# Attention's projections read a transposed copy of x; the layer norm moves into the weights and into row factors

## Chip, core and metric

The kernel runs on one core of one Trainium2 chip. The metric is the time of one execution on the device in microseconds (us), median of the runs shown. Five engines work side by side, each through its own list of instructions in order: PE (matrix products; PEld is its weight load), DVE (vector), ACT (scalar functions), POOL (the second vector engine) and SP (issues all DMAs here). They wait for each other by semaphores.

## The reference

x is 2 x 2048 x 512. The kernel computes one pre-norm block of a transformer:

```
x = x + attention(layernorm(x))      16 heads of 32, rotary positions, causal softmax, Wo
x = x + ffn(layernorm(x))            base_w and base_b, plus 8 low-rank experts, the best 2 of each row
layernorm(x) = (x - mean) / sqrt(var + 1e-5), by row
```

Queries, keys and values are layernorm(x) times Wq, Wk and Wv transposed; queries and keys are then turned by cosine and sine of the position.

## The kernel before

The 4096 rows are worked in 8 blocks of 512 rows (n = 0 to 7, `BLK`), four per batch; a block has four row tiles of 128 (t). The heads are worked in four groups of four (g); a group's 128 columns lie on 128 partitions. A step is one (block, group). In each step PE computes the scores of the next step once for the row maxima (`sm`, L410; reduced on DVE, L428) and the scores of the present step again, transposed (`sc`, L557), with the maxima subtracted by a small product (L581). ACT takes the exponential into `pt` (L597), PE multiplies with the values (`av`, L631), and POOL adds the `pt` tiles up for the row sums (L680). Three `pt` buffers rotate (`PTS`). The sums go through DRAM to be inverted and spread (L701 to L714).

Before a block's attention its projections are made ready by `prepare(n)`: `load` brings the four row tiles (L140) and the cosine and sine of the block (L148); `measured` takes mean and variance on DVE (L181 to L183), and the power -0.5 and the shift on POOL (L184, L185); `scaled` normalises on ACT (L189); `turned` transposes each tile on PE by four products with the identity into one PSUM bank (L195), and ACT copies it to `xnt_a` (L196). `project` (L225) makes one group's keys or queries from `xnt_a`: four products over the 128-row parts c of the weight; then DVE swaps pairs (L238) and multiplies with the cosine (L239), POOL multiplies the swapped with the sine (L240) and adds (L241). `value` (L250) makes one row tile's values, and ACT copies them per group (L258). `finish` does a block's output product, norm, experts and result.

The order on PE, ACT and DVE is the order in which the program emits it (`manual_schedule`, L65); POOL and SP are ordered by the tile framework's scheduler. A planner in the main loop (L864 to L920) counts phases, half a tile of keys for four heads each, some 3 us. `set_aside(at, do)` emits do at a phase; `wait(stage, at, not_before)` puts PE work in a list with a due phase, a cost in us and an earliest phase, which is emitted between attention's products when credit or due time says so. `start_block(n)` is called one block ahead and fixes these phases from the block's first phase `at`, `LEAD` (12, fewer behind a short block) and `EARLY` (14). In it, before the change:

```
set_aside(at - lead - EARLY + t, lambda t=t: load(t))
set_aside(at - lead - EARLY + 2 + t, lambda t=t: measured(t))
set_aside(at - lead - EARLY + 4 + t, lambda t=t: scaled(t))
wait([(0.5, lambda t=t: turned(t))], at - lead - 8 + t, at - lead - 9 + t)
```

Projections may be emitted from phase `at - lead - 6`. Behind blocks 0 and 4, whose causal part is one block wide, lead is 0. `xnt_a`, cosine and sine have one buffer each, the weights of `finish` one buffer `w` in turn, and the tag `tmp` six (row tiles, swapped pairs, sums).

Of the kernel before, what the change touches and what calls it, by code (L numbers as in the profile page):

```python
# [21 lines left out]
BLK = 512  # L22
NT = BLK // P
NB = S // BLK
NC = D // P
EPS = 1e-5
# [8 lines left out]
def preln_attention_moe_lora(  # L35
    ctx: ExitStack,
    tc: tile.TileContext,
    x: bass.AP,
    wq_t: bass.AP,
    wk_t: bass.AP,  # L40
    wv_t: bass.AP,
# [9 lines left out]
    nc = tc.nc  # L51
# [70 lines left out]
    one = const.tile([P, 1], F32, name="one")  # L122
# [3 lines left out]
    power = const.tile([P, 1], F32, name="power")  # L126
# [5 lines left out]
    blocks = [(b, j) for b in range(B) for j in range(NB)]  # L132
# [36 lines left out]
    def load_in_turn(src, name):  # L169
# [2 lines left out]
        nc.sync.dma_start(out=w, in_=src.rearrange("(c p) o -> p c o", p=P))  # L172
        return w

    def moments(xt, t, name):

        n6, n2 = nc.vector.BN_STATS_DIM, nc.vector.BN_AGGR_DIM
        made = small.tile([P, n6 + n2 + 2], F32, tag="mom", bufs=4, name=f"mom_{name}_{t}")
        st, mv = made[:, :n6], made[:, n6 : n6 + n2]
        rstd, shift = made[:, n6 + n2 : n6 + n2 + 1], made[:, n6 + n2 + 1 :]  # L180
        nc.vector.bn_stats(st, xt)  # L181
        nc.vector.bn_aggr(mv, st)
        nc.vector.tensor_scalar_add(rstd, mv[:, 1:2], EPS)  # L183
        nc.gpsimd.tensor_tensor(rstd, rstd, power, ALU.pow)  # L184
        nc.gpsimd.tensor_scalar(shift, mv[:, 0:1], rstd, -1.0, ALU.mult, ALU.mult)  # L185
        return rstd, shift

    def normalise(xn, xt, by):
        nc.scalar.activation(xn, xt, AF.Identity, bias=by[1], scale=by[0])  # L189
# [8 lines left out]
    def prepare(n):  # L198

        j = blocks[n][1]
        made = {"q": [], "k": [], "v": []}
        held = {"x": [], "by": []}

        def load(t):
            held["x"].append(first_x[t] if n == 0 else load_x(n, t, False))
            if t == NT - 1:
                held["turn"] = first_turn if n == 0 else load_turn(j)

        def measured(t):
            held["by"].append(moments(held["x"][t], t, f"a{n}"))

        def scaled(t):
            normalise(held["x"][t], held["x"][t], held["by"][t])

        def turned(t):
            if t == 0:
                held["xn_t"] = wide.tile([P, NC, BLK], F32, tag="xnt_a", name=f"xnt_a{n}")
            turn(held["x"][t], held["xn_t"], t, f"a{n}")  # L220

        def project(which, w, g):
            pj = bank(f"{which}ps_{n}_{g}")
            for c in range(NC):
                nc.tensor.matmul(  # L225
                    out=pj,
                    lhsT=w[:, c, bass.ts(g, P)],
                    rhs=held["xn_t"][:, c, :],
                    start=(c == 0),
                    stop=(c == NC - 1),  # L230
                )
            if which == "k":
                dest = kv.tile([P, BLK], F32, tag="k", name=f"k_{n}_{g}")
            else:
                dest = wide.tile([P, BLK], F32, tag="q", bufs=3, name=f"q_{n}_{g}")
            made[which].append(dest)
            sw = p2.tile([P, BLK], F32, tag="tmp", bufs=6, name=f"sw_{which}_{n}_{g}")
            nc.vector.stream_shuffle(sw, pj, SWAP)  # L238
            nc.vector.tensor_mul(dest, pj, held["turn"][0])  # L239
            nc.gpsimd.tensor_mul(sw, sw, held["turn"][1])  # L240
            nc.gpsimd.tensor_add(dest, dest, sw)  # L241

        def value(t):
            if t == 0:
                made["v"] += [
                    kv.tile([P, NT, P], F32, tag="v", name=f"v_{n}_{g}") for g in range(NC)
                ]
            pv = bank(f"vps_{n}_{t}")
            for c in range(NC):
                nc.tensor.matmul(  # L250
                    out=pv,
                    lhsT=held["xn_t"][:, c, bass.ts(t, P)],
                    rhs=wv[:, c, :],
                    start=(c == 0),
                    stop=(c == NC - 1),
                )
            for g in range(NC):
                nc.scalar.copy(made["v"][g][:, t, :], pv[:, bass.ts(g, P)])  # L258
# [6 lines left out]
        return (load, measured, scaled, turned), heads, [[(3.6, lambda t=t: value(t))] for t in range(NT)], made  # L265

    def finish(n, ctx_t):

# [542 lines left out]
    def set_aside(at, do):  # L811
        aside.append((at, do))
        aside.sort(key=lambda entry: entry[0])

    def wait(stage, at, not_before=0):
        waiting.append((at, len(waiting), not_before, stage))
        waiting.sort(key=lambda entry: entry[:2])

    def start_block(n):

        (load, measured, scaled, turned), heads, vals, made = prepare(n)
        keys[n], values[n], queries[n], contexts[n] = made["k"], made["v"], made["q"], []
        at = begin[NC * n]

        lead = min(LEAD, at - begin[NC * n - 1] - 6) if n > 0 else 0
        for t in range(NT):
            if n > 0:
                set_aside(at - lead - EARLY + t, lambda t=t: load(t))
                set_aside(at - lead - EARLY + 2 + t, lambda t=t: measured(t))
                set_aside(at - lead - EARLY + 4 + t, lambda t=t: scaled(t))  # L830
                wait([(0.5, lambda t=t: turned(t))], at - lead - 8 + t, at - lead - 9 + t)
            else:
                load(t)
        if n == 0:
            for do in (measured, scaled, turned):
                for t in range(NT):
                    do(t)
            make_masks_of_maxima()
        for g in range(NC):
            for i, stage in enumerate(heads[g]):  # L840
                if n == 0 and 2 * g + i < 3:
                    do_stage(stage)
                else:
                    here = begin[NC * n + g]

                    free = begin[NC * n + g - 1] + 3 if i else 0
                    wait(stage, here - 4 + i, max(free, at - lead - 6))
            if g == 1:
                for stage in vals:
                    wait(stage, begin[NC * n + 1] + 1, at - lead - 6)  # L850

    def end_block(n):

# [3 lines left out]
        for i, stage in enumerate(stages):  # L857
            wait(stage, start + (i + 1) * (end - start) / len(stages), start)

    EARLY, BEHIND, LEAD = 14, 3, 12  # L860
    start_block(0)
    before = turned = ending = None
    late = []
    for step in steps + [None]:  # L864
        maxima = []
        if step:
            n, g = step
# [15 lines left out]
        for i in range(slots):  # L883
# [3 lines left out]
            for _ in side_by_side(*todo):  # L887
                phase[0] += 1
                given = between()
# [12 lines left out]
                while available(phase[0]) is not None:  # L902
# [78 lines left out]
```

## Time and profile before

| | us |
|---|---|
| runs | 1808.67 median (1806.64 to 1812.35, 3 runs) |
| profiled execution, its own time | 1807.61 |
| its span, first to last instruction | 1805.6 |
| mean granted clock of TensorE | 0.993 |
| DMA bytes | 61.53 MB, 42284 packets |
| x transposed on PE (L195, 128 products) | 22.1 busy |
| x normalised on ACT (L189) / copied (L196) | 26.3 / 18.4 busy |
| power and shift on POOL (L184, L185) | 17.5 / 8.5 busy |
| POOL's additions of pt (L680) | 1093.0 busy |

Busy time is the time in which an engine had an instruction under way; products on PE overlap, so the sum of their durations is more than their busy time. In a row "a 302" is the mean duration of one instruction in ns. The chain of work that ended last follows the last instruction back from releaser to releaser, so its shares say what the end waited for. Idle time in front of an instruction names the engine that ended it. "xnps_a<-ident,xa" is output and inputs by the program's names.

### The profile page before, as it was taken

How to read it: one execution, taken by the hardware profiler on the slowest of the kernel's cores; microseconds unless marked ns; L12 is line 12 of the kernel's file. 1: busy time of each engine (PE TensorE's matmuls, PEld its weight loads, DVE VectorE, ACT ScalarE, POOL GpSimd, SP SyncE). 2: the span in 40 equal slices, each digit the busy share in tenths (PEclk: the TensorE clock that was granted, in tenths of full speed). 3: DMA queues.
4: the chain of work that ended last, by engine and by line, in shares of the span. 5: the costliest groups of instructions: out<-in, count | busy, mean ns of one | idle time of the engine just before them, and what ended most of it. 6: DMA issues, size and time to landing. Idle time of an engine off the chain costs nothing.

```text
span 1805.6 us, 39826 instructions
## 1 busy us (share of the span) xinstructions
PE 1748.6 (97%) x16568; PEld 757.7 (42%) x16568; DVE 991.3 (55%) x2347; ACT 764.4 (42%) x1600; POOL 1380.7 (76%) x890
## 2 busy tenths in 40 slices
PE   8999999999999999999899999999999999999898
PEld 3544444444443343433344444344444443444334
DVE  4656655566557656562254646465565566565504
ACT  2434433445434535455342424334344445353461
POOL 3647776698788899799984468567996798997971
PEclk9999999999999999999999999999999999999999
DMA  5000101002100001200000122110022000002001
GB/s 187 20 14 20 60 28 51 7 8 72 60 13 7 8 25 42 72 7 2 25 26 13 49 66 60 42 42 4 10 72 66 1 8 7 25 8 72 8 8 47
DMA packets 42284, 61.53 MB, mean 34 GB/s; under 512 B 13180, under 2 KB 13692, under 8 KB 42104
## 3 DMA queue, kind: packets, MB, share of 16 engines
q1 hardware_dynamic: 42104, 59.00, 10.5%
q8 instruction: 129, 2.11, 0.5%
q14 instruction: 51, 0.42, 0.1%
HBM read 50.08 MB, written 8.90 MB: 33 GB/s over the span
## 4 chain that ended last, share of the span: by engine, by line
PE 83%; POOL 6%; issue 5%; DVE 4%; ACT 1%; DMA 0%; SPq 0%; POOLq 0%; DVEq 0%
PE sm L410 17%; PE av L631 13%; PE sc L581 7%; PE sc L557 6%; PE vps L250 6%; PE ops L281 6%; PE yps L364 6%; PE qps L225 6%; PE kps L225 6%; POOL pt L680 4%; PE den L670 2%; PE sc L567 2%; PE yps L371 2%; PE sm L419 1%; PE mid L309 1%
## 5 line engine op out<-in xcount | busy, mean ns | idle before, releaser
L680 POOL TENSOR_TENSOR pt<-pt,pt 128x1024 f32<-128x1024 f32 (+3 forms) x556 | 1093.0, 1991 | 215.5 <-ACT pt L597 207.3
L597 ACT ACTIVATE pt<-sc 128x512 f32<-128x512 f32 (+1 forms) x1152 | 594.3, 573 | 809.3 <-PE sc L557 676.4
L428 DVE TENSOR_REDUCE pm<-sm 128x1 f32<-128x512 f32 (+3 forms) x1280 | 711.3, 604 | 377.5 <-PE sm L410 184.0
L410 PE MATMUL sm<-k,q 32*128 32x512 f32 (+3 forms) x2560 | 653.2, 573 | 2.4 <-ACT xnt_a L196 1.3
L557 PE MATMUL sc<-q,k 32*128 32x512 f32 (+3 forms) x2560 | 560.5, 543 | 0.0
L631 PE MATMUL av<-pt,v 128*32 128x256 f32 (+3 forms) x3352 | 319.8, 458 | 1.8 <-ACT ctx L650 1.4
L410 PEld LDWEIGHTS sm<-k,q 32*128 32x128 f32 x2560 | 247.7, 184 | 36.5 <-issue 14.2
L581 PE MATMUL sc<-max,ones_b 3*128 3x512 bf16 (+3 forms) x1648 | 212.5, 308 | 8.7 <-ACT pt L597 4.7
L557 PEld LDWEIGHTS sc<-q,k 32*128 32x128 f32 x2560 | 207.9, 186 | 2.6 <-issue 1.5
L631 PEld LDWEIGHTS av<-pt,v 128*32 128x32 f32 x3352 | 69.2, 108 | 238.5 <-issue 188.6
L581 PEld LDWEIGHTS <-ones_b 3*128 3x128 bf16 x1648 | 62.7, 91 | 194.1 <-issue 190.4
L225 PE MATMUL kps<-xnt_a,wk 128*128 128x512 f32 x256 | 118.3, 605 | 2.5 <-ACT xnt_a L196 2.5
L225 PE MATMUL qps<-xnt_a,wq 128*128 128x512 f32 x256 | 119.2, 608 | 0.9 <-ACT pt L597 0.9
L281 PE MATMUL ops<-wo,ctx 128*128 128x512 f32 x256 | 117.6, 604 | 1.3 <-DVE three L440 1.3
L250 PE MATMUL vps<-wv,xnt_a 128*128 128x512 f32 x256 | 118.0, 604 | 0.0
L364 PE MATMUL yps<-base_w,xnt_f 128*128 128x512 f32 x256 | 115.9, 595 | 0.0
L567 PEld LDWEIGHTS <-which 32*128 32x128 bf16 x2048 | 39.2, 91 | 136.3 <-issue 107.6
L240 POOL TENSOR_TENSOR sw_q<-sw_q,sin 128x512 f32<-128x512 f32 x32 | 40.7, 1272 | 53.3 <-DVE sw_q L238 53.3
L567 PE MATMUL sc<-past,which 32*128 32x32 bf16 x2048 | 57.8, 174 | 21.2 <-DVE three L440 12.1
L419 PEld LDWEIGHTS <-which_q 32*128 32x128 bf16 x2048 | 65.7, 92 | 25.9 <-issue 17.9
L225 PEld LDWEIGHTS qps<-xnt_a,wq 128*128 128x128 f32 x256 | 46.4, 191 | 67.1 <-issue 59.6
L240 POOL TENSOR_TENSOR sw_k<-sw_k,sin 128x512 f32<-128x512 f32 x32 | 40.8, 1274 | 43.1 <-DVE sw_k L238 43.1
(97 smaller groups left out, 1255.2 us busy)
## 6 DMA issues: line engine op xcount, KB each, us to landing
xa<-in_x SPq DMA_DIRECT2D x32, 256.0 KB
xf<-in_x SPq DMA_DIRECT2D x32, 256.0 KB
wo<-in_wo_t SPq DMA_DIRECT2D x8, 1024.0 KB
base_w<-in_base_wt SPq DMA_DIRECT2D x8, 1024.0 KB
out<-xf SPq DMA_DIRECT2D x32, 256.0 KB
sum<-over SPq DMA_DIRECT2D x124, 64.0 KB
cos<-in_cos SPq DMA_DIRECT2D x8, 256.0 KB
sin<-in_sin SPq DMA_DIRECT2D x8, 256.0 KB
```

The lines of the kernel that those rows point to most:

```text
L225: nc.tensor.matmul(out=pj, lhsT=w[:, c, bass.ts(g, P)], rhs=held["xn_t"][:, c, :], start=(c == 0), stop=(c == NC - 1),)
L250: nc.tensor.matmul(out=pv, lhsT=held["xn_t"][:, c, bass.ts(t, P)], rhs=wv[:, c, :], start=(c == 0), stop=(c == NC - 1),)
L281: nc.tensor.matmul(out=po, lhsT=ctx_t[c][:, bass.ts(t, P)], rhs=held["w"][:, c, :], start=(c == 0), stop=(c == NC - 1),)
L364: nc.tensor.matmul(out=po, lhsT=held["xn_t"][:, c, bass.ts(t, P)], rhs=held["w"][:, c, :], start=(c == 0), stop=False,)
L410: nc.tensor.matmul(out=sc[r][:, some[i]], lhsT=q[rows, bass.ts(ts[i], P)], rhs=keys[c][rows, : wide_of[i]], start=(i == 0), stop=(c != j),)
L428: nc.vector.reduce_max(pm[:, t, r, c : c + 1], sc[r][:, here], axis=AX.X)
L557: nc.tensor.matmul(out=sc[r][:, place(kts[i])], lhsT=keys[jj][rows, bass.ts(tt, P)], rhs=q[rows, low(kts[i]) :], start=first(r), stop=(r n ...
L567: nc.tensor.matmul(out=sc[r][:, at : at + DK], lhsT=which[rows, DK * (3 - c) : DK * (3 - c) + P], rhs=past[rows, :], start=first(r), stop= ...
L581: nc.tensor.matmul(out=sc[r][:, at:end], lhsT=ones_b[rows, :], rhs=s["max"][rows, here : here + end - at], start=first(r), stop=(r in held ...
L597: nc.scalar.activation(pt[:, r, all_of], sc[r][:, all_of], AF.Exp, scale=1.0 / math.sqrt(DK))
L631: nc.tensor.matmul(out=s["av"][rows, lo:hi], lhsT=values[jj][g][:, tt, rows], rhs=pts[kt][:, r, at + lo : at + hi], start=(kt == 0 and lo ...
L680: nc.gpsimd.tensor_add(some, some, pts[kt][:, r : r + 2, place(kt)])
```

## The change

Block 0 is left as it was. In the other blocks:

- x comes a second time from the host as x_t (512 x 4096), and `load_other` brings a block's 512 columns of it, not normalised, straight into the buffer `xnt_a` (1 MB), with cosine and sine behind it. Transposes, their copies and the normalising on ACT are gone.
- The subtraction of the mean goes into the weights: `centre` takes from each of wk, wq and wv its mean over the input rows, once, between block 0's steps. POOL adds the four parts to one (`some`, in the buffer `w`), PE sums over partitions with ones, DVE subtracts. With centred weights x and x minus its mean give the same product.
- The factor rstd = (var + eps)^-0.5 of a row goes behind the product. For keys and queries, where rows lie along the free dimension: `spread` writes the four columns of rstd to DRAM (512 numbers) and reads them back copied to 128 partitions, and `scaled` multiplies cosine and sine by it on POOL. For values, where rows are partitions, ACT's copy takes it as its scale.

In the planner x loads and `measured` come two phases earlier than before, `spread` at phase at - lead - 11, `load_other` at at - lead - 9 and both `scaled` at at - lead - 6.

```
+    def centre(w, name):
+        some = wide.tile([P, NC, D], F32, tag="w", name=f"some_{name}")
+        nc.gpsimd.tensor_add(some[:, :2, :], w[:, :2, :], w[:, 2:, :])
+        nc.gpsimd.tensor_add(some[:, 0, :], some[:, 0, :], some[:, 1, :])
+        def centred():
+            mean = bank(f"mean_{name}")
+            nc.tensor.matmul(
+                out=mean, lhsT=one.to_broadcast([P, P]), rhs=some[:, 0, :],
+                start=True, stop=True,
+            )
+            nc.vector.scalar_tensor_tensor(
+                w, mean.unsqueeze(1).to_broadcast([P, NC, D]), -1.0 / D, w, ALU.mult, ALU.add
+            )
+        return centred
...
+        def load_other():
+            held["turn"] = load_turn(j)
+            held["xn_t"] = wide.tile([P, NC, BLK], F32, tag="xnt_a", name=f"xnt_a{n}")
+            nc.sync.dma_start(
+                out=held["xn_t"],
+                in_=x_t[:, bass.ds(b * S + j * BLK, BLK)].rearrange("(c p) s -> p c s", p=P),
+            )
...
+            nc.vector.bn_stats(both[:, :n6], held["x"][t])
+            nc.vector.bn_aggr(both[:, n6:], both[:, :n6])
+            nc.vector.tensor_scalar_add(rstd, both[:, n6 + 1 : n6 + 2], EPS)
+            nc.gpsimd.tensor_tensor(rstd, rstd, power, ALU.pow)
+        def spread():
+            row = dram.tile([NT, P], F32, name=f"row_{n}")
+            nc.sync.dma_start(out=row.rearrange("t p -> p t"), in_=held["rstd"])
+            held["row"] = p2.tile([P, BLK], F32, tag="tmp", bufs=6, name=f"rows_{n}")
+            nc.sync.dma_start(
+                out=held["row"],
+                in_=row.rearrange("(o t) p -> o (t p)", o=1).to_broadcast([P, BLK]),
+            )
         def scaled(t):
-            normalise(held["x"][t], held["x"][t], held["by"][t])
+            if n == 0:
+                normalise(held["x"][t], held["x"][t], held["by"][t])
+                return
+            nc.gpsimd.tensor_mul(held["turn"][t], held["turn"][t], held["row"])
...
+                    nc.scalar.activation(
+                        made["v"][g][:, t, :], pv[:, bass.ts(g, P)], AF.Copy,
+                        scale=held["rstd"][:, t : t + 1],
+                    )
...
-                set_aside(at - lead - EARLY + t, lambda t=t: load(t))
-                set_aside(at - lead - EARLY + 2 + t, lambda t=t: measured(t))
-                set_aside(at - lead - EARLY + 4 + t, lambda t=t: scaled(t))
-                wait([(0.5, lambda t=t: turned(t))], at - lead - 8 + t, at - lead - 9 + t)
+                set_aside(at - lead - EARLY - 2 + t, lambda t=t: load(t))
+                set_aside(at - lead - EARLY + t, lambda t=t: measured(t))
...
+        if n > 0:
+            set_aside(at - lead - EARLY + 5, load_other)
+            set_aside(at - lead - EARLY + 3, spread)
+            for t in range(2):
+                set_aside(at - lead - 6, lambda t=t: scaled(t))
...
+        if n == 0:
+            for i, w in enumerate((wk, wq, wv)):
+                held = []
+                set_aside(CENTRED + 2 * i, lambda w=w, i=i, held=held: held.append(centre(w, i)))
+                wait([(0.9, lambda held=held: held.pop()())], CENTRED + 2 * i + 2, CENTRED + 2 * i + 1)
...
-    EARLY, BEHIND, LEAD = 14, 3, 12
+    EARLY, BEHIND, LEAD, CENTRED = 14, 3, 12, 4
...
+        "x_t": given("attn_x").reshape(B * S, D).T,
```

More of the change, by code (lines that the diff above doesn't have):

```diff
@@ L38, in preln_attention_moe_lora @@
     x: bass.AP,
+    x_t: bass.AP,
     wq_t: bass.AP,
@@ L202, in prepare @@
         j = blocks[n][1]
+        b = blocks[n][0]
         made = {"q": [], "k": [], "v": []}
@@ L207, in load @@
             held["x"].append(first_x[t] if n == 0 else load_x(n, t, False))
-            if t == NT - 1:
-                held["turn"] = first_turn if n == 0 else load_turn(j)
-        def measured(t):
-            held["by"].append(moments(held["x"][t], t, f"a{n}"))
+            if t == NT - 1 and n == 0:
+                held["turn"] = first_turn
+        def load_other():
[5 more added lines that the diff above has]
+            )
+        def measured(t):
+            if n == 0:
+                held["by"].append(moments(held["x"][t], t, f"a{n}"))
+                return
+            if t == 0:
+                held["rstd"] = small.tile([P, NT], F32, tag="rstd", bufs=1, name=f"rstd_{n}")
+            n6, n2 = nc.vector.BN_STATS_DIM, nc.vector.BN_AGGR_DIM
+            both = small.tile([P, n6 + n2], F32, tag="mom", bufs=4, name=f"mom_a{n}_{t}")
+            rstd = held["rstd"][:, t : t + 1]
+            nc.vector.bn_stats(both[:, :n6], held["x"][t])
[10 more added lines that the diff above has]
+            )
         def scaled(t):
-            normalise(held["x"][t], held["x"][t], held["by"][t])
+            if n == 0:
+                normalise(held["x"][t], held["x"][t], held["by"][t])
+                return
+            nc.gpsimd.tensor_mul(held["turn"][t], held["turn"][t], held["row"])
         def turned(t):
@@ L257, in value @@
             for g in range(NC):
-                nc.scalar.copy(made["v"][g][:, t, :], pv[:, bass.ts(g, P)])
+                if n == 0:
+                    nc.scalar.copy(made["v"][g][:, t, :], pv[:, bass.ts(g, P)])
+                else:
+                    nc.scalar.activation(
+                        made["v"][g][:, t, :], pv[:, bass.ts(g, P)], AF.Copy,
+                        scale=held["rstd"][:, t : t + 1],
+                    )
         heads = [
@@ L264, in prepare @@
         ]
-        return (load, measured, scaled, turned), heads, [[(3.6, lambda t=t: value(t))] for t in range(NT)], made
+        return (load, load_other, measured, spread, scaled, turned), heads, [[(3.6, lambda t=t: value(t))] for t in range(NT)], made
     def finish(n, ctx_t):
@@ L819, in start_block @@
     def start_block(n):
-        (load, measured, scaled, turned), heads, vals, made = prepare(n)
+        (load, load_other, measured, spread, scaled, turned), heads, vals, made = prepare(n)
         keys[n], values[n], queries[n], contexts[n] = made["k"], made["v"], made["q"], []
@@ L850, in start_block @@
                     wait(stage, begin[NC * n + 1] + 1, at - lead - 6)
+        if n == 0:
+            for i, w in enumerate((wk, wq, wv)):
+                held = []
+                set_aside(CENTRED + 2 * i, lambda w=w, i=i, held=held: held.append(centre(w, i)))
+                wait([(0.9, lambda held=held: held.pop()())], CENTRED + 2 * i + 2, CENTRED + 2 * i + 1)
     def end_block(n):
```

## The prediction

> **What bounds the kernel now.** I read first the page's busy shares and its chain of work that ended last:
>
> ```profile
> PE 1748.6 (97%) x16568; PEld 757.7 (42%) x16568; DVE 991.3 (55%) x2347; ACT 764.4 (42%) x1600; POOL 1380.7 (76%) x890
> PE 83%; POOL 6%; issue 5%; DVE 4%; ACT 1%; DMA 0%; SPq 0%; POOLq 0%; DVEq 0%
> ```
>
> TensorE is busy for all but 57 us and is 83% of the chain, so time taken from its stream should come off the end. But POOL is 6%, and the "issue" 5% are mostly gaps between POOL's additions. A share is a mean, so I read next the busy time by stretch (columns: PE, PEld, DVE, ACT, POOL, then PEclk):
>
> ```profile
> 800.00:820.00 20.00, 20.00 (x159) 7.38 (x162) 10.31 (x18) 8.95 (x20) 19.84 (x11) 1.00 0.00 1
> 860.00:880.00 20.00, 17.77 (x128) 5.89 (x127) 4.06 (x8) 8.93 (x20) 19.84 (x11) 1.00 0.15 41
> 880.00:900.00 20.00, 15.06 (x240) 7.97 (x237) 5.97 (x18) 6.85 (x14) 19.92 (x11) 0.88 0.06 15
> 900.00:920.00 20.00, 19.57 (x280) 9.69 (x278) 10.01 (x27) 7.69 (x17) 19.44 (x14) 0.78 0.01 2
> ```
>
> From 860 to 900 POOL is full and PE is not: the additions of pt (L680) set the pace. The chain, read in slices of 15 us, has three such stretches: about 843 to 895, 1500 to 1532 and 1658 to 1711, some 136 us. Elsewhere PE sets the end. PE gains before such a stretch pass through it if POOL had idle time ahead of it; it had 5.8 us at 763 and more before 1500 and 1658.
>
> What the change touches, in the groups by line (count | busy, mean ns | idle before):
>
> ```profile
> L195 PE MATMUL xnps_a<-ident,xa 128*128 128x128 f32 x128 | 22.1, 302 | 8.1 <-ACT xa L189 7.8 <-DVE three L440 0.2
> L189 ACT ACTIVATE xa<-xa,mom_a 128x512 f32<-128x512 f32 x32 | 26.3, 820 | 6.1 <-POOL mom_a L185 5.7 <-DVE mom_a L183 0.2
> L196 ACT COPY xnt_a<-xnps_a 128x512 f32<-128x512 f32 x32 | 18.4, 587 | 7.1 <-PE xnps_a L195 6.9
> L185 POOL TENSOR_SCALAR mom_a<-mom_a 128x1 f32<-128x1 f32 x32 | 8.5, 265 | 3.2
> L240 POOL TENSOR_TENSOR sw_k<-sw_k,sin 128x512 f32<-128x512 f32 x32 | 40.8, 1274 | 43.1 <-DVE sw_k L238 43.1
> ```
>
> **What goes.** In the built program's order the transposes of blocks 1 to 7 are gone: 7 x 16 = 112 of 128, in 28 groups of four. A mean of 302 ns is the length of a pipelined instruction, not its price. The price is the start-to-start distance in PE's timeline:
>
> ```profile
> 74.75 0.60 PE L195 MATMUL xnps_a<-ident,xa 128*128 128x128 f32 x4
> 75.28 0.19 PE L567 MATMUL sc<-past,which 32*128 32x32 bf16 x2
> 221.22 0.66 PE L195 MATMUL xnps_a<-ident,xa 128*128 128x128 f32 x4
> 221.72 0.60 PE L195 MATMUL xnps_f<-ident,xn_f 128*128 128x128 f32 x4
> ```
>
> 75.28 - 74.75 = 0.53 and 221.72 - 221.22 = 0.50; two others gave 0.59 and 0.49. I take 0.53: 28 x 0.53 = **14.8 us** of PE. The waits that the transposes fed go too:
>
> ```profile
> PE xnps_a L195 <- ACT xa L189: 7.8, 1, 7.8
> PE kps L225 <- ACT xnt_a L196: 2.5, 3, 1.1
> PE sm L410 <- ACT xnt_a L196: 1.3, 1, 1.3
> ```
>
> The 7.8 is block 0, which stays, and of the 2.5 block 0 has 1.1. That leaves 1.4 + 1.3 + 0.2 (xnps_a behind three) = **2.9 us**.
>
> ACT loses 28 x (0.82 + 0.587) = 39.4 us. The 112 copies of v (282 ns each) become activations with a scale per row. The nearest rows are L189 (820 ns, two operands per row, from SBUF) and the exponential L597 at 128x512 (573 ns, none), so each costs between 0 and 0.25 us more, at most 28 us. ACT is 42% busy and 1% of the chain: I count 0, and a bank of vps freed up to 4 x 0.25 = 1 us later is covered by seven rotating banks. Uncovered, it would be 28 x 1 us at the worst.
>
> [...]
>
> **What is added once, in block 0.** Three products for the means, each one of the four 128x512 products of a projection. A projection takes 3.63 us on the chain (L225 x8), so 3 x 3.63/4 = **+2.7 us** of PE. DVE gets three corrections of 2048 elements from PSUM. L290 takes 691 ns for 512 and L690 292 for 128, or 1.04 ns an element, so 0.69 + 1536 x 0.00104 = 2.3 us each. Behind them in DVE's order stand row maxima (L428) and a shuffle; POOL gets 3 x (2.36 + 1.27) = 10.9 us, behind which stand sw_q's product and the first additions of pt. From 44 to 92 us DVE is about half busy and POOL 62%, and PE does not use a corrected weight for hundreds of its instructions. I take **+1 us**; with no cover it is 6.9 + 10.9, about +18.
>
> **What is added per block.** The inverse deviations go to DRAM and come back copied to all partitions; then POOL multiplies cosine and sine: 2 x 1.27 us, less 4 x 0.27 for the shift, +1.4 us. POOL stands at the cosine until the row is back. No row of this kernel does that, but the sums' round trip is near it (chain in order of time):
>
> ```profile
> 217.10 0.25 DVE few L707
> 217.38 1.39 DMA over<-few
> 218.78 0.33 SPq L710
> 219.62 0.42 SPq L710
> 220.08 1.97 DMA sum<-over
> ```
>
> One write and one read back: 0.35 for SP's issue, 1.4, 0.4, 2.0, about 4.2 us. The new write is 512 pieces of 4 bytes and the read four times as large, so 4.2 is the lower end; twice it, 8.4, the upper. I take 4.5 by the nearest row. In the built order one to two POOL instructions stand between the last power and the cosine: one addition (2.36 us) in block 4, 1.27 in blocks 3 and 7, more elsewhere. So POOL idles 1 to 3 us per block, and the additions of pt queue behind it; the exponentials wait for those through three pt buffers, and PE for them. POOL has over 10 us idle around the preparations of blocks 1, 2, 3, 6 and 7, so there it costs 0; at 8.4 us it would cost up to 4 each.
>
> [...]
>
> Block 4 is prepared at 764 to 781, where POOL begins the saturated run that ends at 895. It gains 1.4 us of work and waits 4.5 - 2.36 = 2.1. POOL has 5.3 us of idle in that run after 768, so part is absorbed: **+1 us**. And with POOL that full I do not count block 4's own four transposes as a gain: **+2.1**.
>
> The transposed x is 1 MB on SP's queue, into the one buffer that the former block's last query projection reads. A load of that size (base_w, issued at 415.20) had moved its bytes by 420, so about 5 us. In blocks 2, 3, 4, 6 and 7 the first projection comes at least three phases of some 3 us later, and hides it. In blocks 1 and 5 it does not: in block 5 the query projection ended at 928.45 and the key projection started at 937.83. Less four transposes (2.1) and 0.9 of waits, 6.5 us are left for 5.2 of load, but in SP's order the load stands behind the row's write and read, which wait for POOL's power. I take 1 us late in each, **+2**; with nothing hidden, 5 us each, +10. The cosine and sine, loaded behind it, are needed scaled when the first projection ends, 3.6 us later; DVE's first product of the block waits for POOL there with row maxima behind it. I count that in the same 1 us.
>
> At nothing I cost the planner's reshuffle (the same projections and outputs stand a few phases apart; eight products of values with weights are split in more pieces), the x loads two phases earlier, and the sums in the buffer of wo and base_w: wo's first load waits for the third mean, over 50 us before its first use.
>
> **The sum.** -14.8 - 2.9 + 2.7 + 1 + 1 + 2.1 + 2 = -8.9 us. The profiled execution took 1807.61 us (span 1805.6, 2.0 around it), so 1798.7 by its own time. The median, 1808.67, is 1.1 higher. I predict **1799**.
>
> **Rivals.**
> - *All of it is gained.* The load and the round trip hide everywhere and POOL's stretches only shift: -14.8 - 2.9 + 2.7 = -15, or 1793, and to 1787 if less clock is lost: PEclk 0.88 and 0.78 above are 2.4 + 4.4 = 6.8 us at half speed right after POOL's stretch, which may move. For it: 97% of PE.
> - *The gain goes into new waits.* The loads of blocks 1 and 5 fully seen (+8 over my 2) or the centring seen (+6): 1804 to 1810. For it: SP issues in order, and its queue already waits for xf, sums and base_w.
> - *Slower: the round trip stops POOL.* If the row takes 8.4 us or is issued late behind another's wait, POOL stands 4 to 6 us in each of seven blocks with the additions of pt behind it, the pt buffers come free that much later, and ACT and then PE run dry. Each us of it that reaches PE costs 7 in all: at 1.3 per block the gain of 8.9 is gone, from 2.1 (14.7 - 8.9 = +5.8, 1813) the kernel is slower, and at the 4 us of the upper bound it is 28 - 8.9 = +19, or 1827. For it: POOL is 76% busy and full in the heavy blocks. Against it: POOL waited 17.6 us for the sums' DMA in all (L714), and PE lost nothing that is put down to it.
>
> That the change does not do what it says I give nothing: the built order shows the transposes gone.
>
> **How the numbers follow.** Forecast (1794 to 1803) 0.43; all gained (1786 to 1794) 0.14; gain eaten (1803 to 1814) 0.22; slower (above 1814) 0.21. A measurement of this kernel tells 0.3% (5.4 us) from no change: faster means below 1803.2, slower above 1814.1. So 0.57, 0.22, 0.21. The range, 1788 to 1818, leaves out about 0.05 below and 0.13 above; of the round trip it takes in 2.7 us per block ((1818 - 1799)/7).
>
> **What would show it.** Right: PE busy about 12 us lower; no xnps_a in blocks 1 to 7; ACT 11 to 39 us lower, POOL about 21 higher (+10.9 + 7 x 1.4). "PE kps <- DMA xnt_a" at most 2 to 3 us. POOL cos <- DMA rows 1 to 3 us per block. Wrong: POOL's wait for rows over 5 us in a block with ACT pt <- POOL behind it; PE waits for xnt_a over 3 us; DVE's k <- POOL cos wait followed by PE waits for a bank.

## The result, and the profile after

The changed kernel takes 1870.82 us in the median (1867.39 to 1873.59, 5 runs), beside 1808.67 of the kernel before (1806.63 to 1812.35, 5 runs): a ratio of 1.0337 with an interval of 1.0315 to 1.0358. It is slower by about 62 us; 1799 was forecast, and the range ended at 1818. The profiled execution took 1867.39 us (span 1865.6).

The changed kernel's page, busy shares and chain by engine:

```profile
PE 1754.5 (94%) x16510; PEld 752.7 (40%) x16510; DVE 999.2 (54%) x2350; ACT 742.1 (40%) x1544; POOL 1400.8 (75%) x882
PE 74%; issue 9%; POOL 8%; DVE 4%; DMA 3%; ACT 1%; SPq 0%; POOLq 0%; DVEq 0%; ACTq 0%
```

PE's idle time, span less busy, went from 57.0 to 111.1 us (+54.1). PE's busy time rose by 5.9 although the transposes are gone. DMA, which had 0% of the chain, has 3%, POOL two points more. Its groups by line, for what the change touched (count | busy, mean ns | idle before):

```profile
L214 PE MATMUL xnps_a<-ident,xa 128*128 128x128 f32 x16 | 3.9, 419 | 19.5 <-ACT xa L208 19.5
L312 ACT ACTIVATE v<-vps,rstd 128x128 f32<-128x128 f32 x112 | 32.0, 370 | 72.4 <-PE vps L301 72.4
L266 POOL TENSOR_TENSOR cos<-cos,rows 128x512 f32<-128x512 f32 x7 | 8.9, 1265 | 81.1 <-DMA rows<-row 46.0 <-DMA cos<-in_cos 23.3 <-DMA sums<-sum 11.7
```

16 transposes are left of 128, so the change does what it says. But POOL stood 81.1 us ahead of seven cosines, 11.6 each (the row factors, the cosine itself and the sums, all on SP's queue, are named as what came last), and block 0's transposes waited 19.5 us in place of 7.8. The main waits of PE that are new or grown, in all of the changed kernel, and ACT's wait for POOL (total us, times, longest):

```profile
PE xnps_a L214 <- ACT xa L208: 19.5, 1, 19.5
PE xnps_f L214 <- ACT xn_f L208: 11.9, 2, 10.7
PE kps L276 <- DMA xnt_a<-in_x_t: 11.8, 2, 6.2
PE sc L638 <- DVE pm L485: 7.1, 1, 7.1
PE sm L467 <- POOL q L292: 4.3, 1, 4.3
PE den L727 <- POOL pt L737: 4.9, 2, 2.8
ACT pt L654 <- POOL pt L737: 75.9, 25, 14.5
```

Beside the start, the waits of 10.7, 11.8, 7.1 and 4.3 are the largest, and each lies where a block is prepared. The last two rows are POOL's additions of pt, late behind its stand: ACT's row was 58.4 before, its longest wait 5.1. First the timeline of block 3's preparation, POOL's lines, then SP's (start, duration, what; in brackets the idle time before):

```profile
498.92 0.55 POOL L251 TENSOR_TENSOR rstd<-rstd,power 128x1 f32<-128x1 f32 x1
500.58 1.27 POOL L737 TENSOR_TENSOR pt<-pt,pt 128x512 f32<-128x512 f32 x1 [1.11 <-ACT pt L654]
513.96 1.27 POOL L266 TENSOR_TENSOR cos<-cos,rows 128x512 f32<-128x512 f32 x1 [12.11 <-DMA rows<-row]
```

```profile
499.49 0.38 SPq L255 DMA_DIRECT2D row<-rstd  x1
508.36 0.33 SPq L257 DMA_DIRECT2D rows<-row  x1
```

The last power ends at 499.47, the cosine starts at 513.96: the round trip is 14.5 us, where I took 4.5 and bounded it by 8.4. The write alone takes from 499.49 to 508.36, and in that time SP, which issues in order, stands at the load of the rows with every other transfer behind it. In all seven blocks the write takes 8.7 to 11.3 us.

SP's stand costs by itself. In block 4 (SP's lines, then DVE's):

```profile
807.41 0.38 SPq L255 DMA_DIRECT2D row<-rstd  x1
816.08 0.33 SPq L257 DMA_DIRECT2D rows<-row  x1
816.50 1.12 SPq L758 DMA_DIRECT2D sums<-sum  x4
```

```profile
810.70 1.29 DVE L485 TENSOR_REDUCE pm<-sm 128x1 f32<-128x512 f32 x2 [0.89 <-PE sm L467]
823.18 0.25 DVE L764 RECIPROCAL few<-few 128x16 f32<-128x16 f32 x1 [11.19 <-DMA few<-sums]
```

The sums of an earlier step, which have nothing to do with the change, are issued at 816.50 instead of near 808; DVE stands 11.19 us at their reciprocal, row maxima stand behind it, and PE waits 7.1 us for them (the row above). In blocks 1 and 5 the load of the transposed x stands there (PE's 11.8). In block 6 POOL's 11.19 us at the cosine delay the powers of the second norm, and PE waits 10.7 for `xn_f`.

The late start is in POOL's timeline of the changed kernel's first 20 us:

```profile
10.69 2.34 POOL L179 TENSOR_TENSOR some<-wk 128x1024 f32<-128x1024 f32 x1 [8.98 <-DMA wk<-in_wk_t]
17.72 0.55 POOL L203 TENSOR_TENSOR mom_a<-mom_a,power 128x1 f32<-128x1 f32 x1 [0.35 <-DVE mom_a L202]
```

The built order of POOL, which the scheduler sets, has the sum of wk ahead of the causal mask (12.98, before at 2.19) and of block 0's powers. It waits 9 us for the 1 MB weight, and the first power comes at 17.72 instead of 6.00.

Last, the clock. By stretch of the changed kernel around the preparation of block 5 (columns: PE, PEld, DVE, ACT, POOL busy, then PEclk):

```profile
960.00:980.00 20.00, 17.33 (x266) 9.00 (x270) 9.08 (x23) 6.34 (x14) 13.57 (x14) 0.91 0.03 3
980.00:1000.00 20.00, 14.34 (x107) 5.93 (x108) 5.17 (x17) 2.88 (x7) 9.88 (x9) 0.74 0.39 107
1000.00:1020.00 20.00, 20.00 (x216) 9.32 (x214) 8.17 (x19) 8.27 (x19) 11.24 (x9) 1.00 0.07 15
```

From 980 to 1000, where PE waits 5.6 us for the transposed x, its granted clock is 0.74; the clock's records have half speed there from 982.2 to 992.4, and the eight products of a projection that start at 989.38 take 5.19 us, beside 3.70 for the eight from 949.10 on, at full clock. The mean clock was 0.993 before and is 0.981 after: 12.6 and 35.4 us of full clock lost. That fits a busy time that rose with less work.

### The profile page after: what moved, and what is told of

Same layout as the page of the kernel before. It is cut to its first block, busy times and chain, and to the rows that moved or that the text cites. A ratio compares the mean times of both kernels' runs of the same rounds, so it can differ in the third digit from the quotient of the medians.

```text
span 1865.6 us, 39682 instructions
## 1 busy us (share of the span) xinstructions
PE 1754.5 (94%) x16510; PEld 752.7 (40%) x16510; DVE 999.2 (54%) x2350; ACT 742.1 (40%) x1544; POOL 1400.8 (75%) x882
## 4 chain that ended last, share of the span: by engine, by line
PE 74%; issue 9%; POOL 8%; DVE 4%; DMA 3%; ACT 1%; SPq 0%; POOLq 0%; DVEq 0%; ACTq 0%
PE sm L467 15%; PE av L688 11%; PE ops L338 6%; PE sc L638 6%; POOL pt L737 6%; PE sc L614 5%; PE vps L301 5%; PE kps L276 5%; PE yps L421 5%; PE qps L276 5%; PE den L727 2%; PE sc L624 1%; PE mid L366 1%; PE yps L428 1%; DMA row<-rstd 1%
## 5 line engine op out<-in xcount | busy, mean ns | idle before, releaser
L467 PE MATMUL sm<-k,q 32*128 32x512 f32 (+3 forms) x2560 | 658.2, 575 | 10.5 <-DVE three L497 5.6
L276 PE MATMUL kps<-xnt_a,wk 128*128 128x512 f32 x256 | 122.6, 623 | 12.9 <-DMA xnt_a<-in_x_t 11.8
L276 PEld LDWEIGHTS kps<-xnt_a,wk 128*128 128x128 f32 x256 | 47.8, 196 | 74.4 <-issue 69.7
L476 PE MATMUL sm<-past_q,which_q 32*128 32x32 bf16 x2048 | 71.2, 173 | 5.3 <-issue 5.3
```

What stands on the lines that cost most here:

```text
L276: nc.tensor.matmul(out=pj, lhsT=w[:, c, bass.ts(g, P)], rhs=held["xn_t"][:, c, :], start=(c == 0), stop=(c == NC - 1),)
L467: nc.tensor.matmul(out=sc[r][:, some[i]], lhsT=q[rows, bass.ts(ts[i], P)], rhs=keys[c][rows, : wide_of[i]], start=(i == 0), stop=(c != j),)
L476: nc.tensor.matmul(out=sc[r][:, at : at + DK], lhsT=which_q[rows, DK * (3 - m) : DK * (3 - m) + P], rhs=past_q[rows, :], start=False, stop ...
```

## The experiments

The theory: the loss is the late landing of the row factors' 4-byte write and the late start, and PE's pauses cost clock beside themselves. The rivals differ by run: POOL's stand at the rows alone, many pieces instead of small ones, a loss that belongs to the change as a whole. Letters in an expectation are that run's own. Ratios are to the kernel before, run beside them (median 1808.67 for the changed kernel, 1811.5 for e_best and e_both16, 1811.0 for the others); they come from all runs and differ a little from the quotient of the medians. Idle and busy time and clock are those of the profiled execution.

| run | median us | ratio | PE idle | PE busy | clock |
|---|---|---|---|---|---|
| changed kernel | 1870.82 | 1.0337 (1.0315 to 1.0358) | 111.1 | 1754.5 | 0.981 |
| e_dve_sum | 1859.06 | 1.0273 (1.0256 to 1.0290) | 94.5 | 1757.7 | 0.982 |
| e_no_wait | 1853.27 | 1.0236 (1.0219 to 1.0253) | 88.6 | 1761.8 | 0.982 |
| e_no_hold | 1836.58 | 1.0136 (1.0118 to 1.0154) | 76.6 | 1758.4 | 0.983 |
| e_row16 | 1816.98 | 1.0034 (1.0021 to 1.0047) | 68.7 | 1746.4 | 0.990 |
| e_row512 | 1814.35 | 1.0017 (1.0007 to 1.0027) | 68.2 | 1745.0 | 0.991 |
| e_both | 1805.55 | 0.9973 (0.9963 to 0.9984) | 59.4 | 1743.8 | 0.990 |
| e_both16 | 1810.07 | 0.9994 (0.9984 to 1.0004) | 64.3 | 1748.4 | 0.989 |
| e_best | 1807.93 | 0.9980 (0.9969 to 0.9991) | 58.0 | 1745.5 | 0.991 |
| b_centre | 1828.69 | 1.0096 (1.0076 to 1.0116) | 69.3 | 1753.5 | 0.992 |
| p_pause | 1878.34 | 1.0372 (1.0355 to 1.0389) | 111.9 | 1765.8 | 0.975 |

### The start: e_dve_sum and b_centre

```
-        nc.gpsimd.tensor_add(some[:, :2, :], w[:, :2, :], w[:, 2:, :])
-        nc.gpsimd.tensor_add(some[:, 0, :], some[:, 0, :], some[:, 1, :])
+        nc.vector.tensor_add(some[:, :2, :], w[:, :2, :], w[:, 2:, :])
+        nc.vector.tensor_add(some[:, 0, :], some[:, 0, :], some[:, 1, :])
```

> The changed kernel with the four parts of each weight added on DVE instead of POOL. Theory (the late start of 11.7 us comes from POOL: the centring of wk waits there for 1 MB, ahead of the causal mask and of block 0's powers): the first transpose is back at about 8 us and the time falls by 11 to 14 us, to about 1858. Rival (the start is late because of what is loaded, or the loss is all in the blocks): the first transpose stays at 19.5 us and the time within 3 us of 1871.

Measured 1859.06, 11.8 us less; the first transposes wait 7.8 us again. DVE's order is the emitted one, so the sums stand where the program put them.

The kernel before with `centre` and its call alone:

> The kernel before with the centring of the three weights alone (sums on GpSimd as in the change; the values and keys are the same, as the rows are already centred). Theory A (the centring of the first weight is taken up on GpSimd ahead of the causal mask and the factors of block 0, waits there for its 1 MB load, and the first transposes come 11.7 us later; three products and the corrections add 0 to 3): 1820 to 1824 us, ratio 1.006 to 1.0085, first transposes wait 19 to 20 us. Rival B (the late start belongs to the change as a whole, for instance to its other loads, or is caught up within block 0): 1808 to 1812.

Measured 1828.69, ratio 1.0096, some 17 us, more than either theory said; the first transposes wait 19.2 us. PE's idle time is 12.3 us more (the start), its busy time 4.9 more: 3.4 is the row of the three products, and the rest fits the half-clock time, 27 us in place of 24. So the late start is the centring's own and isn't caught up.

### The round trip: who stands at it

e_no_wait: POOL multiplies by a constant tile instead of `rows`; all transfers stay.

```
-            nc.gpsimd.tensor_mul(held["turn"][t], held["turn"][t], held["row"])
+            nc.gpsimd.tensor_mul(held["turn"][t], held["turn"][t], bias_sb[:, :BLK])
```

> The changed kernel with all its DMAs, but POOL multiplies cosine and sine by a constant tile that has long been there (the bias) instead of the row factors, so keys and queries lack their factors. Theory (POOL standing at the cosine for the row, with pt's additions behind it, is the main loss in the blocks): POOL's waits of 11 to 12 us go in blocks 2, 3, 4, 6, 7, PE's pauses there too; the start (11.7) and the waits for the transposed x in blocks 1 and 5 (11.8) stay: 1818 to 1835. Rival (the load of x, SP's queue or the planner's order cost it, POOL only shows it): within 8 us of 1871.

Measured 1853.27: a miss, far above the 1818 to 1835 expected, and 17.6 us under the changed kernel. The trace of this run says where the rest is. Waits of SP and POOL, of DVE and of PE (total, times, longest):

```profile
SPq L257 <- DMA row<-rstd: 60.6, 7, 9.8
POOL ctx L771 <- DMA sum<-over: 48.1, 15, 12.6
POOL cos L266 <- DMA cos<-in_cos: 25.2, 4, 13.0
```

```profile
DVE few L764 <- DMA few<-sums: 40.4, 4, 24.6
```

```profile
PE kps L276 <- DMA xnt_a<-in_x_t: 9.7, 2, 5.2
PE sc L638 <- DVE pm L485: 7.0, 1, 7.0
```

SP still stands 60.6 us at the load, though nobody uses what it brings, and PE waits for the transposed x and for row maxima nearly as in the changed kernel. (Of DVE's 40.4, 11.0 are block 4's; the 24.6 lie near the end, where the kernel before has 28.4.) POOL no longer waits for the rows, but still for what SP brings late: 25.2 us for the cosine, loaded behind the rows, and 48.1 for the sums, 22.6 in the changed kernel. These waits of POOL fall from 81.1 + 22.6 to 73.3 us only, so 17.6 isn't the price of all of POOL's standing.

e_no_hold: the same, and the load of the rows is left out, so SP doesn't stand.

```
-            nc.sync.dma_start(
-                out=held["row"],
-                in_=row.rearrange("(o t) p -> o (t p)", o=1).to_broadcast([P, BLK]),
-            )
```

> The changed kernel in which the row factors are still written as 512 pieces of 4 bytes, but nobody reads them: the load of the rows is left out, and GpSimd multiplies cosine and sine by a constant tile, so that keys and queries lack their row factors. Beside the run that also multiplied by a constant but kept the load of the rows (1853.27) it shows whether the write costs by being waited for on SyncE's queue. Theory A (SyncE stands at the load until the write has landed, and the load of the transposed x, the sums and their way back stand behind it): with no load nothing stands, 1812 to 1819 us, ratio 1.001 to 1.005. Rival B (512 small pieces themselves hold up the transfers behind them or the other engines): 1840 to 1853, ratio over 1.016.

Measured 1836.58, between the two: 16.7 us less, for SP's hold and, not separated from it, the load itself (256 KB a block). Some 20 us stay although the write is waited for by nobody. SP's timeline of this run, at block 2, then at block 4:

```profile
240.55 0.38 SPq L255 DMA_DIRECT2D row<-rstd  x1
241.03 0.45 SPq L760 DMA_DIRECT2D over<-few  x1
251.91 1.72 SPq L762 DMA_DIRECT2D sum<-over  x4
```

```profile
798.26 0.38 SPq L255 DMA_DIRECT2D row<-rstd  x1
798.69 1.24 SPq L753 DMA_DIRECT2D sums<-sum  x4
807.59 0.34 SPq L756 DMA_DIRECT2D few<-sums  x1
```

`over<-few`, 1.39 us in the trace of before, takes from 241.03 to 251.91 when it is issued half a microsecond behind the row's write; the sums' four writes take till 807.59, where before no wait for them was over 1.3 us. So a transfer that is issued just behind the write lands 9 to 11 us after its issue, about when the write itself does in the changed kernel. Taken away one after the other, POOL's wait for the rows gives 17.6 us, SP's hold 16.7, and larger pieces the last 19.6 (1836.58 to e_row16's 1816.98). The three overlap, as POOL also waits for what SP holds up; taken away in another order, each could come out otherwise.

### The write in larger pieces: e_row16 and e_row512

e_row16 writes 128 pieces of 16 bytes (the rows then hold the factors in another order):

```
-            row = dram.tile([NT, P], F32, name=f"row_{n}")
-            nc.sync.dma_start(out=row.rearrange("t p -> p t"), in_=held["rstd"])
+            row = dram.tile([P, NT], F32, name=f"row_{n}")
+            nc.sync.dma_start(out=row, in_=held["rstd"])
```

> The changed kernel with the row factors written to DRAM in 128 pieces of 16 bytes instead of 512 of 4, and read back as they lie, so the factors stand in another order than the rows. Theory A (the number of pieces makes the write late): the write lands in 2 to 4 us instead of 8.7 to 11.2, 1835 to 1850. Theory B (pieces below some size between 16 and 64 bytes complete late however few): still 8 us or more, and within 6 us of 1871. Rival (it is the wait for other DMAs on the queue): no change either way.

e_row512 transposes rstd on PE and writes 4 pieces of 512 bytes, `spread` two phases later:

```
+            tp = bank(f"rsps_{n}")
+            nc.tensor.transpose(tp[:NT, :P], held["rstd"], ident)
+            flat = p2.tile([P, BLK], F32, tag="tmp", bufs=6, name=f"flat_{n}")
+            nc.scalar.copy(flat[:NT, :P], tp[:NT, :P])
+            nc.sync.dma_start(out=row, in_=flat[:NT, :P])
```

> The changed kernel with the row factors transposed on PE (128x4 to 4x128) and copied by ACT, so that the row is written in 4 pieces of 512 bytes; two phases later. Theory: the write lands in about 1.5 us as the sums' 64-byte and 2 KB writes do, POOL's wait per block falls from 11.5 to 2 to 5 us, SP gets to the transposed x earlier, and the time is 1825 to 1842, the start still late. Rival (a round trip over DRAM in front of POOL is too long in any form): 1850 or more.

Measured 1816.98 and 1814.35, both better than expected, by 18 and 11 us: what the write does to other transfers had not been counted. SP's timeline at block 3 of e_row16:

```profile
483.69 0.33 SPq L255 DMA_DIRECT2D row<-rstd  x1
486.21 0.33 SPq L257 DMA_DIRECT2D rows<-row  x1
```

The write lands in 2.5 us; in e_row512 it is 1.7 there (487.83 to 489.56), where the changed kernel takes 8.9. PE's busy time falls by 8 to 10 us against the changed kernel with the same products (seven small transposes more in e_row512), as its time at half clock falls, from 72 us to 38 and 34.

### The landing by itself: p_pieces and p_landing

p_pieces put writes of a constant into the kernel before:

> The kernel before with writes of a constant put into SyncE's queue, one every 13 phases, each with a small load behind it that waits for its landing; nothing else uses them. Five forms in turn: 512 pieces of 4 bytes, 512 of 16, 512 of 64, 128 of 4, 128 of 16. It measures the disputed landing by itself. Theory A (the number of pieces sets the landing): the three forms with 512 pieces each hold SyncE 8 to 11 us, the two with 128 pieces 1.4 to 2.6. Rival B (the size of a piece does, 4 bytes being dear): 512 pieces of 4 bytes 8 to 11, 128 of 4 some 2.5 to 4, the three others 1.4 to 3. The time is not what is looked for; SyncE's holds alone may make it up to 1850.

It failed as a measurement: as the constant is ready at once, the scheduler put every write into the first 100 us of SP's queue (1860.78 us, one execution), and the waits behind them say nothing on one landing. p_landing takes the writes' source from the block's own normalised rows:

```
+        nc.sync.dma_start(out=to.rearrange("t p -> p t"), in_=src[:, :4])
+        nc.sync.dma_start(out=dram.tile([1, 16], F32, name=f"back_a{told[0]}"), in_=to[:1, :16])
```

> The kernel before with 28 writes out of the normalised x of blocks 1 to 7, one as each of the 28 groups of rows is ready, in SyncE's queue, each with a small transfer behind it that reads what was written and so waits for its landing; nothing else uses them. Five forms in turn: a) 512 pieces of 4 bytes, b) 512 of 16, c) 128 of 4, d) 128 of 16, e) a) and then d), with the wait for d) alone. The transfers depend on the block's own rows, so that they can't be put at the kernel's start as in the probe before. Theory A (the number of pieces sets the landing): a) and b) hold SyncE 7 to 11 us, c) and d) 1.4 to 2.6. Rival B (4-byte pieces are dear): a) 7 to 11, b) 1.5 to 3, c) 2.5 to 4, d) 1.4 to 2.6. In both, if a later transfer lands only with the earlier one, e) holds 7 to 11 us, otherwise 1.4 to 2.6. The time is not what is looked for.

SP's timeline in this run, the first of each form (a to d), then one of e:

```profile
73.62 0.38 SPq L866 DMA_DIRECT2D to_a<-xa  x1
81.90 0.56 SPq L867 DMA_DIRECT2D back_a<-to_a  x1
82.56 0.54 SPq L871 DMA_DIRECT2D to_b<-xa  x1
86.69 0.65 SPq L872 DMA_DIRECT2D back_b<-to_b  x1
89.20 0.38 SPq L876 DMA_DIRECT2D to_c<-xa  x1
96.89 0.51 SPq L877 DMA_DIRECT2D back_c<-to_c  x1
98.86 0.34 SPq L881 DMA_DIRECT2D to_d<-xa  x1
101.30 0.59 SPq L882 DMA_DIRECT2D back_d<-to_d  x1
...
225.03 0.38 SPq L886 DMA_DIRECT2D to_e<-xa  x1
225.45 0.50 SPq L888 DMA_DIRECT2D next<-xa  x1
235.35 0.60 SPq L889 DMA_DIRECT2D back_e<-next  x1
```

From issue to the end of the wait: a) 512 x 4 bytes 8.3 us (8.3 to 10.5 where nothing else held SP), b) 512 x 16 bytes 4.1 (2.6 to 4.1), c) 128 x 4 bytes 7.7 (6.8 to 8.2), d) 128 x 16 bytes 2.4 (2.4 to 3.4 where no 4-byte write went ahead), e) d) behind a) 9.9 (9.0 to 11.3); the run took 1850.85 us in one execution. The number of pieces, Theory A, falls: 512 pieces of 16 bytes are quick. The size decides, and more sharply than Rival B had it: even 128 pieces of 4 bytes take 7 to 8 us. And e) shows that a later transfer lands late behind the 4-byte write, about when a) lands alone.

### The clock: p_pause

The kernel before with a stop in PE's queue at each block change:

```
+            tp = bank(f"stop_{n}")
+            nc.tensor.transpose(tp[:, :P], ident, ident)
+            nc.scalar.copy(some[:, :P], tp[:, :P])
+            for _ in range(STOPS):
+                nc.scalar.copy(some[:, :P], some[:, :P])
+            tp = bank(f"go_{n}")
+            nc.tensor.transpose(tp[:, :P], some[:, :P], ident)
```

> The kernel before with a pause put into TensorE's queue at each of the 7 block changes: a transpose, 21 copies of 128x128 on ScalarE one after the other, and a second transpose of what they leave; nothing else uses it. 21 copies of some 0.25 to 0.3 us make a pause of 5 to 6.5 us, 7 of them 37 to 45. Theory A (a pause costs itself and a stretch at half clock after it, of one to three steps of 3.4 us, so 1.7 to 5 more per pause): TensorE at half clock for 24 us in the kernel before, for 48 to 95 here; time 1858 to 1885. Rival B (the clock's half stretches in the changed kernel have another cause than its pauses, so a pause costs itself alone): half clock stays near 24 us, time 1846 to 1854.

What PE waited for there, and the stretches after the stop of block 3 (it ends at 489.78):

```profile
PE go L834 <- ACT some L832: 51.9, 7, 7.7
```

```profile
489.80:497.00 7.20, 6.29 (x13) 2.69 (x13) 0.89 (x3) 0.27 (x1) 0.00 (x0) 0.79 0.00 0
497.00:504.00 7.00, 6.05 (x87) 3.89 (x89) 4.17 (x14) 3.68 (x8) 3.87 (x6) 0.69 0.25 78
```

The stops are 51.9 us (7.4 each), the kernel is 67 us slower. Idle time rose by 54.9, busy time by 17.2 for 14 added transposes. The mean clock is 0.975: 46.9 us of full clock lost, against 12.6. At most 5.6 of the busy time are the added transposes (2.3 and 3.3 in their rows), so a pause of 7.4 us costs 1.7 to 2.5 us more in slow products. In the clock's records PE was at half speed for 24 us before, 72 in the changed kernel and 92 here (behind the start, and without each run's last 1 us), always in whole steps of 3.4 us. The runs don't show that one long pause is needed for such a stretch. In the kernel before, the longest is

```profile
895.20:908.80 13.60, 13.12 (x140) 6.07 (x140) 4.11 (x9) 6.03 (x13) 13.44 (x8) 0.50 0.01 2
```

with PE busy in nearly all of it. From 880 to 895 PE was busy for 10.75 of 15.2 us, and its longest wait was 2.8.

### Both mends: e_both, e_both16, e_best

> The changed kernel with both mends: the row factors written as four pieces of 512 bytes, and the sums of the centring on VectorE. Theory A (the change loses by two things alone, the late landing of the 4-byte write and the late start, and the two add up): the 512-byte kernel's 1814.35 less the 11.8 that the VectorE sums gave on the changed kernel (1870.8 to 1859.06), 1802.5 us, ratio 0.995 to 0.998, first transposes wait 7.8 us as in the kernel before. Rival B (the centring costs as much wherever its sums stand, since VectorE is later for block 0): 1808 or more, ratio at or over 1. Rival C (something else in the change still costs, and what was won at the start is waited for later in block 0): 1808 to 1814.

Measured 1805.55, ratio 0.9973: faster than the kernel before by some 5 us (0.3%), and by 65 than the changed kernel. It lies between Theory A's 1802.5 and Rival C's 1808. Its page:

```profile
PE 1743.8 (97%) x16517; PEld 747.7 (41%) x16517; DVE 1005.4 (56%) x2356; ACT 744.4 (41%) x1551; POOL 1392.1 (77%) x876
PE 84%; DVE 5%; POOL 4%; issue 4%; ACT 1%; DMA 1%; SPq 0%; POOLq 0%; DVEq 0%; ACTq 0%
```

PE is at 97% again, idle for 59.4 us; the start gave back 8.8 of the 11.8 us expected. The first transposes' wait fell by 11.1 us (18.9 in e_row512, 7.8 here), so some of it is waited for later, as Rival C had it.

> The changed kernel with the sums of the centring on VectorE and the row factors written as 128 pieces of 16 bytes, without the transpose and copy that the 512-byte form takes (the rows then hold the factors in another order, so keys and queries get other rows' factors). Its landing was 1.4 to 2.5 us in the run that had only this mend (1816.98). If the two mends add, 1816.98 less 11.8 is 1805, ratio 0.996 to 0.998, the same as the 512-byte form with VectorE sums; if the way of writing still costs beside its landing, 1808 or more.

Measured 1810.07: here the start gave 6.9, and the 16-byte form is 0.2% behind the 512-byte one. With only the write mended it lands in 2.5 us at block 3 of e_row16 and in 1.7 at block 3 of e_row512; whether that has to do with the difference wasn't tried.

e_best puts e_both's two products by the rows on VectorE (`nc.vector.tensor_mul` in `scaled`):

> The version with both mends, and cosine and sine multiplied by the row factors on VectorE, which is busy 56% of the time, in place of GpSimd, which is busy 77%. Theory A (of the 59 us for which TensorE still stands there, the 4.2 us at the start of block 5 are GpSimd's lateness with the queries, and go): 14 products of 1.27 us leave GpSimd, some 18 us, 1800 to 1804, ratio 0.994 to 0.997. Rival B (VectorE, first in the chain at a block's start, stands at the rows and is late with the maxima): 1806 to 1815, ratio 0.998 to 1.003.

Measured 1807.93, in Rival B's range, ratio 0.9980 with an interval that overlaps e_both's. PE's wait of 4.2 us for POOL's queries in block 5 is gone, and PE's waits for DVE's `three` ahead of `sm` rose from 5.6 to 8.6 us. Nothing is won; e_both stays the best.

## Why the prediction was wrong

- **The bound on the round trip failed: "4.2 is the lower end; twice it, 8.4, the upper", and 4.5 taken.** It is 14.5 us in block 3. The row that I took as nearest, `over<-few`, writes pieces of 64 bytes; its 1.4 us says nothing of 4-byte pieces, which p_landing puts at 7 to 10 us (6.8 to 10.5) beside 2.4 to 4.1 for 16 bytes. I named the 512 pieces of 4 bytes and widened the bound for them by a factor that had no row behind it. The step in the landing lies between 4 and 16 bytes: 16 bytes (1.4 to 2.5 us in e_row16) are about as quick as 512 (1.2 to 3.2 in e_row512).
- **"There it costs 0" in blocks 1, 2, 3, 6 and 7 failed.** POOL's idle time there was real, but the stand is 11 to 12 us in each of the seven blocks, more than it, and block 5 had no term for it at all. And it isn't only POOL's wait for the rows: my slower rival had the right case, with +19 us as its worst, but only 17.6 of the write's 53.8 us (1870.82 less 1816.98) went with that wait, the rest with SP's hold and with the late landing of other transfers. I had counted SP's order for the load of x_t alone. "PE lost nothing that is put down to it" was said of the sums' own trip, which takes 1.4 us for `over<-few` in the trace of before and 10.9 behind the row's write (e_no_hold, block 2); e) of p_landing agrees, 9.0 to 11.3 us for a write that takes 2.4 to 3.4 alone. What it waits for in that time, no run here shows.
- **The centring's "+1" failed.** By e_dve_sum it is 11.8 us, by b_centre some 17, the three products among them. What cost is not its 10.9 us of POOL work, for which I had looked for cover from 44 to 92 us, but its place, as the first transposes' wait shows, 19.5 and 7.8 us: POOL is ordered by the scheduler, and the built order had the first sum ahead of the mask. I read that order for the blocks' preparations and not for the start.
- **A term was missing: clock.** I had priced lost clock only as something that may move (6.8 us). A pause of PE costs slow products behind it, 1.7 to 2.5 us for one of 7.4 (p_pause). After the change PE has 12.1 us less work (14.8 transposes less 2.7 products) and yet 5.9 us more busy time, 18 us in all, beside 22.8 us more of full clock lost.
- **The load of x_t, "1 us late in each", +2,** was 6.2 and 5.6 us, but only behind the row's write: with the write mended PE waits 0.3 us for it (e_row512).
- **Right:** the transposes' gain and the means. PE's busy time in e_both fits them: 12.1 less, but 2.0 for the seven small transposes and 5.4 of full clock lost again, leaves 4.7, and 4.8 less is measured. The 2.9 us of waits were not won on balance: PE's idle time is 59.4 us there, 57.0 before, with a new wait of 4.2 for POOL's queries. Right too: ACT 22.3 us lower (11 to 39 forecast), POOL 20.1 higher (21 forecast). The copies of v became 88 ns dearer (282 to 370), and no new wait of PE is put down to them.
- **Two slips in the working change nothing:** 937.83 - 928.45 less 2.1 and 0.9 leaves 6.4 us, not 6.5, and the 6.8 us read from PEclk are full clock lost, so 13.6 us at half speed.

With the write's pieces and the place of the sums mended, the forecast's gain is there in part: 0.9973, some 5 us of the 8.9.

## What to carry to other kernels

A small write's landing went by the size of its pieces, 6.8 to 10.5 us for 4 bytes and 2.4 to 4.1 for 16, and less by their number, 6.8 to 8.2 for 128 pieces of 4 bytes and 8.3 to 10.5 for 512 (p_landing): take a row with the same piece size, or leave the bound open, and put numbers that lie one per partition side by side before they are written. The slow transfer here cost whoever waited for it (17.6 us with POOL's wait), whatever stood behind it in the queue (16.7 with SP's hold), and whatever was issued just behind it on other business (some of the last 19.6); look at each of the three. Where a scheduler orders an engine, read the built order at the start too, and price each pause of PE above its own length (here 1.7 to 2.5 us more for one of 7.4).

## What the hardware showed that was not expected

- Writes to DRAM in 4-byte pieces land 6.8 to 8.2 us after issue with 128 of them and 8.3 to 10.5 with 512; 16-byte pieces in 2.4 to 4.1 (p_landing), or 1.4 to 2.5 (e_row16). Sizes between were not tried.
- A 2 KB write of 16-byte pieces that is issued 0.4 us behind a 4-byte one lands after 9.0 to 11.3 us. Why 4-byte pieces land late stays open: no run here shows what they do in that time.
- Seven pauses of 7.4 us each cost 67 us and not 52; TensorE was at half clock for 92 us in place of 24 (p_pause).
- TensorE also went to half clock, for 13.6 us, after waits of which none was over 2.8 us (the kernel before, 895 to 909).
